# Forward transform of the last 64 rows: two matmuls on two quarters of the array become four matmuls on four quarters

## The chip, the core and the metric

The kernel runs on one core of a Trainium2 chip. The metric is the device time of one execution in microseconds (us); lower is better. Everything is float32. The engines go by the names of the profile: PE is the matrix engine (PEld its weight loads), DVE, ACT and POOL the vector, scalar and general engines, SP the engine that issues most DMAs. The array of PE is 128 rows by 128 columns. A matmul whose contraction has 64 rows and whose result has 64 rows fills a quarter of it; which quarter follows from the partitions that its inputs lie on and from those that its result goes to.

## What is computed

The reference runs two layers on an image batch `x` of 2 x 128 x 64 x 64. The first is a neighbourhood attention with layer norms and a small feed-forward part. The second is a full self-attention over the 4096 tokens of a batch, then a layer norm, and then a convolution over time with 16 long filters per branch, plus three short lags:

```
t = t + attention(ln(t))                         # 4096 tokens, 128 channels
u = ln(t)
U_plus, U_minus = causal FFT convolution of u with 16 filters   # per branch
t = t + sum_k s_k (U_plus_k @ M_plus_k + U_minus_k @ M_minus_k) + sum_i shift(u, i) @ M_u_i
```

One of four branches is chosen by a one-hot weighting, and the branches see the first 1, 1/2, 1/4 or 1/8 of the tokens.

## The kernel before

The convolution is done in blocks with a real transform of length `NC` = 320 (`CB` = 256 and `SB` = 64). The rows of the spectrum go through DRAM: the forward transform writes them to the buffer `us`, and the last stage loads them as `ut`. Beside `us` there is `gs` with the transformed filters.

The stages follow each other on the timeline like this:

- Up to about 440 us: the first layer, planned by hand, and the first work of the second.
- About 440 to 1332 us: the attention of batch 0 and then of batch 1, in `attention`. Its inner loop has PE do the products of tokens (L897), which ACT turns into weights `e` (L904); the weighted sums (L925, L950); and transposes of `e` (L911), which DVE copies out with their row sums to `et` (L914) before L925 takes them. After each inner step `fill()` puts in a slice of other work: the queue `urgent` first, then `steps`.
- About 1332 us to the end: the products in the transformed domain (L1304, L1316) and the way back.

Each time a chunk of 512 tokens has its final sum, `fill` gets a new generator `after` for it; there are 8 for each batch. Its slices are: transposes of the sum (L974), with a normalisation by DVE into `tt` (L979); the layer norm (L159, POOL's L160, and L177, which writes `z`); transposes of `z` (L188), copied by ACT into `zc` (L990); two slices with two matmuls each for the first 256 of the 320 rows of the transform (L1010), copied out by DVE and ACT in turn (L1012) and stored (L999); and a last slice for the remaining 64 rows (L1018, L1020), which is what the change touches. In batch 1's last steps, slices of `short_lags` (L1042, with DVE's L1049 and ACT's L1033) lie between.

In each slice `z2` holds 128 partitions. The two halves of 64 partitions, `q`, are two segments that are transformed separately; the transform matrix `tr` lies on both halves.

The buffers around the change: PSUM tiles `bank` come from a ring of six (`ps_m`) which all of these users share; the SBUF tiles `ub` come from a ring of three, and each `after` takes five of them; in the stage from about 838 to 920 us `filter_matrices` loads 32 blocks through two buffers `st` (L1103), which DVE scales and adds (L1106, L1108) and combines (L1119 to L1124). DVE's, ACT's and SP's queues are in order; the framework's scheduler sets that order in the attention stages.

Of the kernel before, what the change touches and what calls it, by code (L numbers as in the profile page):

```python
# [8 lines left out]
F32 = mybir.dt.float32  # L9
# [5 lines left out]
P = 128  # L15
# [66 lines left out]
SB = CB // SG  # L82
NC = CB + SB
# [9 lines left out]
def kernel(  # L93
# [16 lines left out]
    nc = tc.nc  # L110
# [14 lines left out]
    for c in range(4):  # L125
# [19 lines left out]
        out=flip, in_=flip, compare_op=ALU.not_equal, fill=1.0, base=1 - QT * QT, pattern=[[0, 2], [1, QT * QT]],  # L145
# [35 lines left out]
    def layernorm(dst, src):  # L181

        ln_apply(dst, src, ln_statistics(src))

    def transposed(ps, src):

        for j in range(src.shape[1]):
            nc.tensor.transpose(ps[:, j * P : (j + 1) * P], src[:, j, :], ident)  # L188
# [30 lines left out]
    with l0a:  # L219
# [6 lines left out]
        sp = l0a.enter_context(tc.tile_pool(name="l0_s", bufs=2))  # L226
# [27 lines left out]
        def table(ci, h, eng):  # L254
# [16 lines left out]
            out=gavg, in_=gavg, compare_op=ALU.is_ge, fill=0.0, base=0,  # L271
# [3 lines left out]
            out=gavg, in_=gavg, compare_op=ALU.is_ge, fill=0.0, base=3,  # L275
# [8 lines left out]
        for r in range(QT):  # L284
# [4 lines left out]
            rows_ = rev[r * QT : (r + 1) * QT].rearrange("p h n m -> p (h n) m")  # L289
# [563 lines left out]
    us = dram.tile([BINS, 2, SG, FB, NB, 2, P], F32, name="us")  # L853
    gs = dram.tile([BINS, 2, SG, GROW], F32, name="gs")

    with ap_:
        tp = ap_.enter_context(tc.tile_pool(name="l1_t", bufs=1, side="right"))
        ep = ap_.enter_context(tc.tile_pool(name="l1_e", bufs=8, side="right"))
        sp = ap_.enter_context(tc.tile_pool(name="l1_s", bufs=2, side="right"))
# [3 lines left out]
        def bank():  # L863
            return ps_m.tile([P, 512], F32, tag="bank", name="bank")
# [3 lines left out]
        tr = tp.tile([P, 2, NC], F32, name="tr")  # L868
# [98 lines left out]
        def after(b, c, part):  # L967

            n0 = 4 * c
            ph, f0 = divmod(n0, FB)  # L970
            par, h = divmod(ph, 2)
            pt = bank()
            for j in range(4):
                nc.tensor.transpose(pt[:, j * P : (j + 1) * P], xa[b][:, (n0 + j) * P : (n0 + j + 1) * P], ident)  # L974
            rden = sp.tile([P, 4], F32, tag="rden", name="rden")
            nc.vector.tensor_reduce(rden, part[:, n0 : n0 + 4, :], AX.X, ALU.add)
            nc.vector.reciprocal(rden, rden)
            for j in range(4):
                nc.vector.scalar_tensor_tensor(  # L979
                    tt[b][:, n0 + j, :], pt[:, j * P : (j + 1) * P], rden[:, j : j + 1], tt[b][:, n0 + j, :],  # L980
                    ALU.mult, ALU.add,
                )
            yield
            z = sp.tile([P, 4, P], F32, tag="z4", name="z4")
            layernorm(z, tt[b][:, n0 : n0 + 4, :])
            yield
            pt = bank()
            transposed(pt, z)
            s0 = 1 + h * (TH // 2)
            nc.scalar.copy(  # L990
                zc[:, par, s0 : s0 + TH // 2].rearrange("p (c f) -> p f c", f=FB)[:, f0 : f0 + 4, :],
                pt.rearrange("p (f c) -> p f c", f=4),
            )
            yield
            z2 = z.rearrange("p f d -> p (f d)")

            def store(m0, q, src):
                mn = min(P, NC - m0)
                nc.sync.dma_start(  # L999
                    out=us[m0 // 2 : (m0 + mn) // 2, :, 2 * h + q, f0 : f0 + 4, b, par, :].rearrange(  # L1000
                        "g r f d -> (g r) f d"
                    ),
                    in_=src.rearrange("p (f d) -> p f d", d=P),
                )

            for m0 in (0, P):
                for q in range(2):
                    rows_ = slice(q * SB, (q + 1) * SB)
                    pu = bank()
                    nc.tensor.matmul(pu, lhsT=tr[rows_, h, m0 : m0 + P], rhs=z2[rows_], start=True, stop=True)  # L1010
                    ub = sp.tile([P, 512], F32, tag="ub", name="ub", bufs=3)
                    (nc.scalar.copy if q else nc.vector.tensor_copy)(ub, pu)  # L1012
                    store(m0, q, ub)
                yield
            pu = bank()
            for q in range(2):
                rows_ = slice(q * SB, (q + 1) * SB)
                nc.tensor.matmul(pu[rows_], lhsT=tr[rows_, h, 2 * P : NC], rhs=z2[rows_], start=True, stop=True)  # L1018
            ub = sp.tile([P, 512], F32, tag="ub", name="ub", bufs=3)
            nc.scalar.copy(ub, pu)  # L1020
            for q in range(2):
                store(2 * P, q, ub[q * SB : (q + 1) * SB])
            yield

        def short_lags(b, h):
# [154 lines left out]
        def filler(b, steps, kept=None):  # L1180

            urgent, done = [], []

            def fill(c=None, part=None):
                if c is not None:
                    done.append(c)
                    urgent.append(after(b, c, part))
                    if len(done) % 4 == 0:
                        held = kept if kept is not None and len(done) == 4 else urgent
                        held.append(short_lags(b, len(done) // 4 - 1))  # L1190
                    return
                for queue in (urgent, steps):
                    while queue:
                        if next(queue[0], 0) is None:
                            return
                        queue.pop(0)

            return fill, urgent
# [291 lines left out]
```

## Time and profile before

| | |
|---|---|
| Median of 5 runs | 2244.25 us (2243.41 to 2245.45) |
| Profiled execution | 2244.14 us, its span 2242.4 us |
| PE busy | 2174.1 us, 97% of the span |
| DVE, ACT, POOL busy | 940.3, 780.5, 275.8 us |
| Mean granted PE clock | 0.99 |
| L1010 | 128 records of 64x512, 589 to 1219 ns |
| L1018 | 64 records of 64x512, 589 to 641 ns |
| L1012 | 32 copies by DVE (691 ns), 32 by ACT (585 ns) |
| L1020 | 16 copies by ACT (585 ns) |
| L999 | 64 stores of 256 KB, 32 of 128 KB |

How to read it: a float32 matmul of the program appears as two records, and matmuls that lie in different parts of the array overlap, so that records' durations don't add up; the distance between starts does. Ends of matmuls are modelled. In lines of the timeline, the first number is the start in us from the beginning of the span, the second the length in us up to the last end, then come engine, line, operation and tiles, and in brackets the idle time of the engine before it and what ended it. An engine with a q behind its name is its sequencer, which waits or issues.

### The profile page before, as it was taken

How to read it: one execution, taken by the hardware profiler on the slowest of the kernel's cores; microseconds unless marked ns; L12 is line 12 of the kernel's file. 1: busy time of each engine (PE TensorE's matmuls, PEld its weight loads, DVE VectorE, ACT ScalarE, POOL GpSimd, SP SyncE). 2: the span in 40 equal slices, each digit the busy share in tenths (PEclk: the TensorE clock that was granted, in tenths of full speed). 3: DMA queues.
4: the chain of work that ended last, by engine and by line, in shares of the span. 5: the costliest groups of instructions: out<-in, count | busy, mean ns of one | idle time of the engine just before them, and what ended most of it. 6: DMA issues, size and time to landing. Idle time of an engine off the chain costs nothing.

```text
span 2242.4 us, 31648 instructions
## 1 busy us (share of the span) xinstructions
PE 2174.1 (97%) x11888; PEld 1344.9 (60%) x11888; DVE 940.3 (42%) x3046; ACT 780.5 (35%) x1908; POOL 275.8 (12%) x353
## 2 busy tenths in 40 slices
PE   5899998999999999999999999999999999999998
PEld 3677775544454444544544447677677676767677
DVE  4799985434443346433333352222222323232323
ACT  2789883222332223222222332322322323232322
POOL 3367874200000000000000000000000000000000
PEclk8999998999999999999999999999999999999999
DMA  4222222011000016100000132212212122221101
GB/s 109 70 61 61 61 56 51 1 62 56 24 24 24 16 39 178 36 24 19 5 24 24 47 93 55 58 42 56 59 41 57 43 55 49 49 51 47 43 7 76
DMA packets 174810, 109.53 MB, mean 49 GB/s; under 512 B 26049, under 2 KB 159809, under 8 KB 174146
## 3 DMA queue, kind: packets, MB, share of 16 engines
q1 hardware_dynamic: 171818, 105.24, 17.9%
q10 hardware_dynamic: 2840, 2.27, 0.4%
q8 instruction: 94, 1.54, 0.3%
q14 instruction: 58, 0.48, 0.1%
HBM read 72.87 MB, written 34.60 MB: 48 GB/s over the span
## 4 chain that ended last, share of the span: by engine, by line
PE 86%; DVE 6%; POOL 3%; DMA 3%; ACT 1%; issue 1%; SPq 1%; DVEq 0%; ACTq 0%; POOLq 0%
PE acc L1316 25%; PE pc L1304 13%; PE bank L897 9%; PE own L925 9%; PE other L950 8%; PE bank L911 4%; PE bank L331 2%; PE py L1343 2%; PE bank L188 2%; PE bank L541 2%; PE bank L1042 1%; PE bank L1010 1%; DMA st<-in_m_minus_dram 1%; PE po L563 1%; DMA st<-in_m_plus_dram 1%; PE bank L505 1%
## 5 line engine op out<-in xcount | busy, mean ns | idle before, releaser
L1305 DVE COPY y<-pc 128x512 f32<-128x512 f32 x320 | 221.6, 692 | 351.5 <-PE pc L1304 347.8
L904 ACT ACTIVATE e<-bank 128x512 f32<-128x512 f32 x288 | 171.9, 597 | 553.3 <-PE bank L897 418.1
L897 PE MATMUL bank<-cm 128*128 128x512 f32 x576 | 298.6, 602 | 1.4 <-DVE y L652 1.4
L1316 PE MATMUL acc<-y,mpl 128*128 128x256 f32 x1280 | 292.1, 382 | 0.0
L1316 PE MATMUL acc<-y,mmi 128*128 128x256 f32 x1280 | 288.0, 379 | 0.0
L1304 PE MATMUL pc<-ct,ut 64*128 64x512 f32 x1280 | 285.2, 595 | 0.9 <-issue 0.9
L1316 PEld LDWEIGHTS acc<-y,mpl 128*128 128x128 f32 x1280 | 238.1, 190 | 59.4 <-issue 29.6
L1316 PEld LDWEIGHTS acc<-y,mmi 128*128 128x128 f32 x1280 | 242.6, 190 | 32.6
L1305 ACT COPY y<-pc 128x512 f32<-128x512 f32 x320 | 204.6, 639 | 87.2 <-PE pc L1304 87.2
L925 PE MATMUL own<-et,tok 128*128 128x512 f32 x448 | 227.1, 594 | 2.5 <-DVE part L914 2.5
L950 PE MATMUL other<-e,tok 128*128 128x512 f32 x448 | 228.6, 592 | 0.0
L914 DVE CUSTOM_DVE_ANT_0 et<-bank,one 128x512 f32<-128x512 f32 x224 | 145.6, 688 | 166.4 <-PE bank L911 166.3
L1304 PEld LDWEIGHTS pc<-ct,ut 64*128 64x128 f32 x1280 | 121.5, 187 | 145.8 <-issue 140.6
L1322 ACT COPY ob<-acc 128x256 f32<-128x256 f32 x40 | 23.8, 595 | 431.2 <-PE acc L1316 431.2
L925 PEld LDWEIGHTS own<-et,tok 128*128 128x128 f32 x448 | 84.4, 190 | 110.7 <-issue 72.1
L950 PEld LDWEIGHTS other<-e,tok 128*128 128x128 f32 x448 | 85.0, 190 | 106.6 <-issue 106.2
L1355 DVE TENSOR_TENSOR xa<-py,xa 128x512 f32<-128x512 f32 x32 | 22.1, 691 | 281.4 <-PE py L1343 281.4
L897 PEld LDWEIGHTS bank<-cm 128*128 128x128 f32 x576 | 95.7, 193 | 73.8 <-issue 44.7
L911 PEld LDWEIGHTS bank<-ident,e 128*128 128x128 f32 x896 | 103.5, 142 | 57.2 <-issue 43.4
L160 POOL TENSOR_TENSOR ln_rs<-ln_rs,mhalf 128x4 f32<-128x4 f32 x24 | 24.3, 1011 | 848.4 <-DVE ln_rs L159 848.4
L528 ACT ACTIVATE p<-p,mn 128x196 f32<-128x196 f32 x256 | 114.4, 449 | 21.5 <-DVE mn L518 13.4
L911 PE MATMUL bank<-ident,e 128*128 128x128 f32 x896 | 117.8, 275 | 0.0
(199 smaller groups left out, 2311.9 us busy)
## 6 DMA issues: line engine op xcount, KB each, us to landing
ut<-us SPq DMA_DIRECT2D x80, 256.0 KB
us<-ub SPq DMA_DIRECT2D x64, 256.0 KB
vw<-vd SPq DMA_DIRECT2D x256, 49.0 KB
ct<-gs SPq DMA_DIRECT2D x160, 72.0 KB
ct<-gs SPq DMA_DIRECT2D x160, 64.0 KB
gs<-sum SPq DMA_DIRECT2D x20, 256.0 KB
vd<-v SPq DMA_DIRECT2D x128, 32.0 KB
st<-in_m_plus_dram SPq DMA_DIRECT2D x16, 256.0 KB
```

What stands on the lines that cost most here:

```text
L188: nc.tensor.transpose(ps[:, j * P : (j + 1) * P], src[:, j, :], ident)
L331: nc.tensor.matmul(pl, lhsT=wg[:, lo : lo + P], rhs=zT, start=True, stop=True)
L528: nc.scalar.activation(p, p, AF.Exp, bias=t[name + "mn"][:, h : h + 1], scale=-1.0, accum_out=t["den"][:, u, h : h + 1],)
L897: nc.tensor.matmul(ps, lhsT=cm[b][:, n * P : (n + 1) * P], rhs=cm[b][:, chunk(c)], start=True, stop=True)
L904: nc.scalar.activation(e, ps, AF.Exp, bias=0.0, scale=ASCALE, accum_out=part[:, n, c : c + 1])
L911: nc.tensor.transpose(pt[:, k * P : (k + 1) * P], es[k][:, m * P : (m + 1) * P], ident)
L914: nc.vector.tensor_tensor_reduce(et, pt, one, 1.0, 0.0, ALU.mult, ALU.add, part[:, n, a : a + 1])
L925: nc.tensor.matmul(own, lhsT=tok[b][:, n, :], rhs=e, start=first, stop=last)
L950: nc.tensor.matmul(other, lhsT=tok[b][:, 4 * CHUNKS[a] + j, :], rhs=es[j], start=(j == 0), stop=(j == 3))
L1304: nc.tensor.matmul(pc, lhsT=ut[fp, b, par, :], rhs=cv_[fp], start=True, stop=True)
L1305: (nc.scalar.copy if f else nc.vector.tensor_copy)(y[:, 4 * f : 4 * f + 4, :, par, b * 2 * FB + q : (b + 1) * 2 * FB : 2], pc.rearrange("p ...
L1316: nc.tensor.matmul(acc, lhsT=(mmi if l else mpl)[:, k, :], rhs=y[:, 1::2, k, ::-1, :] if l else y[:, 0::2, k, :, :], start=(l == 0 and k = ...
```

## The change

Before, the last slice of `after` runs one matmul for each half `q`: 64 rows in, 64 rows out, 512 columns moving. The result of `q` goes to the partitions of `q` of one bank. ACT copies the bank to one `ub`, and two stores of 128 KB send it off.

After, each matmul is split in two by its moving columns (`i`: 256 columns each). The result of `i` goes to the partition half `i`, and that of `q` to a bank of its own, so that the four matmuls lie in the four quarters of the array. Two banks are taken in place of one. Half of the `ub` is copied by DVE (`q` = 0), the other half by ACT (`q` = 1), with 256 columns each, and four stores of 64 KB follow. The arithmetic is the same.

```diff
-                mn = min(P, NC - m0)
...
-            pu = bank()
-            for q in range(2):
-                rows_ = slice(q * SB, (q + 1) * SB)
-                nc.tensor.matmul(pu[rows_], lhsT=tr[rows_, h, 2 * P : NC], rhs=z2[rows_], start=True, stop=True)
-            ub = sp.tile([P, 512], F32, tag="ub", name="ub", bufs=3)
-            nc.scalar.copy(ub, pu)
-            for q in range(2):
-                store(2 * P, q, ub[q * SB : (q + 1) * SB])
+            banks = [bank() for q in range(2)]
+            for i in range(2):
+                for q in range(2):
+                    rows_ = slice(q * SB, (q + 1) * SB)
+                    nc.tensor.matmul(
+                        banks[q][i * 64 : (i + 1) * 64, 0:256], lhsT=tr[rows_, h, 2 * P : NC],
+                        rhs=z2[rows_, i * 256 : (i + 1) * 256], start=True, stop=True,
+                    )
+            ub = sp.tile([P, 512], F32, tag="ub", name="ub", bufs=3)
+            for q in range(2):
+                (nc.scalar.copy if q else nc.vector.tensor_copy)(ub[:, q * 256 : (q + 1) * 256], banks[q][:, 0:256])
+                for i in range(2):
+                    nc.sync.dma_start(
+                        out=us[P:, :, 2 * h + q, f0 + 2 * i : f0 + 2 * i + 2, b, par, :].rearrange("g r f d -> (g r) f d"),
+                        in_=ub[i * 64 : (i + 1) * 64, q * 256 : (q + 1) * 256].rearrange("p (f d) -> p f d", d=P),
+                    )
```

The order of the instructions on PE and POOL is otherwise the same. On DVE and SP the scheduler's order also changes from about 850 to 920 us: three pairs of L914 and some neighbours stand at other places among the operations of `filter_matrices`.

## The prediction

> **What bounds the kernel now.** I read the page first, for the bound and the chain of waits; then the lines that the change touches; then the timeline of one step, of the two places where PE waits for DVE, and of the only other line that uses parts of the array in both directions.
>
> ```profile
> PE 2174.1 (97%) x11888; PEld 1344.9 (60%) x11888; DVE 940.3 (42%) x3046; ACT 780.5 (35%) x1908; POOL 275.8 (12%) x353
> ...
> PE 86%; DVE 6%; POOL 3%; DMA 3%; ACT 1%; issue 1%; SPq 1%; DVEq 0%; ACTq 0%; POOLq 0%
> ```
>
> PE is busy for 97% of the span and carries 86% of the chain: time taken off PE reaches the end wherever PE does not then wait for something that has not moved. The timeline of the first step:
>
> ```profile
> 483.68 1.07 PE L1018 MATMUL bank<-z,tr 64*64 64x512 f32 x4
> ...
> 484.69 0.98 PE L911 MATMUL bank<-ident,e 128*128 128x128 f32 x7
> 484.85 0.58 ACT L1020 COPY ub<-bank 128x512 f32<-128x512 f32 x1 [0.75 <-ACT e L904]
> 485.38 0.69 DVE L914 CUSTOM_DVE_ANT_0 et<-bank,one 128x512 f32<-128x512 f32 x1 [2.82 <-PE bank L911]
> ```
>
> A float32 matmul is two records (x4 for two matmuls). The two matmuls lie in the two diagonal quarters and run together; from their start to that of L911 PE spends 1.01 us. There are 16 such steps, starting at 483.7, 584.5, 661.4, 722.9, 783.8, 820.7, 848.0, 870.6, 976.1, 1061.1, 1134.2, 1195.2, 1244.1, 1281.0, 1301.4 and 1314.9.
>
> **The matmuls.** A column streams in 0.855 ns (the chain has 64 records of L1316, 256 columns each, in 14.01 us: 0.219 each). So 1.01 = 2 passes x 512 columns (0.876) + 0.13 for changing the array's division and the second weights. After: if all four quarters run at once, 2 passes x 256 columns (0.438) + the overhead. Nearest row, from the timeline of the first layer:
>
> ```profile
> 36.50 0.59 PE L505 MATMUL bank<-kT,qT 32*64 32x196 f32 x16
> 37.02 0.38 PE L720 MATMUL bank<-v_sb,w_sb 128*128 128x1 f32 x2
> ```
>
> Eight matmuls on four row groups x two column groups, each pair on the same rows with other moving data and the other half of one bank, as in the change. PE gets to L720 after 0.52 us. Two passes of 196 columns are 0.335, so the overhead is 0.18; taking turns on the same rows would need four passes, 0.67 of streaming alone. So they run at once. With overheads of 0.13 (L1018) to 0.18 (L505) the step becomes 0.57 to 0.62; I take 0.59, with twice L1018's loads but half of L505's: 0.42 saved, bounds 0.39 to 0.44. Over 16 steps, 6.7 us if all of it arrived.
>
> The Trainium skill's page "TensorE: Matmul & The Clock Gate", section "Part 3: Packing small matmuls — row/col tiling", speaks against this: a weight load overlaps running matmuls only when its row group differs. By it the two column quarters of one row half would take turns, and the sum would be that of the first rival below. The L505 row disagrees.
>
> **Evictions and stores.** Removed: 16 ACT copies (585 ns). Added: 16 ACT and 16 DVE copies of half the size, ACT at most 585, DVE between 341 (L177, 128 columns) and 691 (L1012, 512); I take 460, with 0.37 until the next may start. ACT and DVE are busy 35% and 42%. In an ordinary step the DVE half would run at about 484.4 and be done before L914, which in the changed order comes next and could start at 484.96: nothing while it is ready, and a late copy would delay L914 and the L925 behind it. SP gets 32 issues more, at 0.36 to 0.61 each; SP is idle in most of this stage, so they cost something only where loads queue behind them (below). Each step takes one bank more of the ring of six. In the order of the changed program the nearest misses are L1018's second bank (freed 0.65 before use, 1301.4) and L1042 at 1305.90 (freed 1.02 before), against 0.42 by which PE comes earlier: no stall.
>
> **The new wait.** The fifth ub of a step reuses the buffer of its second, so it waits for that store. Until now only ACT waited. Now the DVE half waits in front of everything queued on DVE. By the semaphore updates that store lands about 5.1 us after the step's first L1010, 483.70 in the first step, before the matmuls end; in the steps at 584.5 and 1061.1 it lands 1.5 later, which holds L914 by 0.2, against 1.1 of slack: nothing. In the step at 1301.4 the matmuls come early and the store late:
>
> ```profile
> 1301.39 1.08 PE L1018 MATMUL bank<-z,tr 64*64 64x512 f32 x4
> ...
> 1303.53 1.13 DVE L979 SCALAR_TENSOR_TENSOR tt<-bank,rden,tt 128x128 f32<-128x128 f32 x4 [1.94 <-PE bank L974]
> ...
> 1305.05 0.58 ACT L1020 COPY ub<-bank 128x512 f32<-128x512 f32 x1 [0.17 <-DMA us<-ub]
> ...
> 1307.17 1.12 DVE L177 TENSOR_SCALAR z<-tt,ln_mv,ln_rs 128x128 f32<-128x128 f32 x4
> ...
> 1308.48 0.60 PE L188 MATMUL bank<-ident,z 128*128 128x128 f32 x4
> ```
>
> In the changed order the DVE half stands ahead of L979. If the store lands as here, 1305.0, L979 starts at 1305.36, 1.83 late; L159, POOL and z follow, z at 1309.0, and the fourth L188 leaves PE 1.46 later than now. This landing is 3.7 after issue where most take 2.8; with 2.8 it is 1304.0, L979 0.87 late, the fourth L188 0.50 late. I take +0.5; bounds -0.42 (nothing held) and +1.5. That step's saving is gone either way.
>
> **838 to 920, the filter matrices.** 32 loads go through two st buffers; DVE takes each, and the next load waits for that:
>
> ```profile
> 850.16 0.75 DVE L1108 SCALAR_TENSOR_TENSOR mmi<-st,wt,mmi 128x512 f32<-128x512 f32 x1 [1.14 <-DMA st<-in_m_minus_dram]
> 851.72 0.75 DVE L1108 SCALAR_TENSOR_TENSOR mmi<-st,wt,mmi 128x512 f32<-128x512 f32 x1 [0.81 <-DMA st<-in_m_minus_dram]
> ...
> 858.67 1.10 PE L188 MATMUL bank<-ident,z 128*128 128x128 f32 x4 [2.95 <-DVE z L177]
> ```
>
> PE waits for z here, so the saving of the step at 848.0 is lost. The changed order also moves work. (a) The DVE half, 0.26 net ahead of L1119, and one L1124 of 0.20 now behind L979: z 0.06 later. (b) SP issues four stores (0.65 apart), the first behind the DVE half (852.9, now 851.47): the next st load goes out at 855.5 for 852.84, but DVE wants it at 859.7; inv at 858.6 for 855.94, so L1272 waits until about 862.3, hidden behind L1012, which needs PE until 862.7. (c) Behind the next step the four stores put one load 1.75 late, and three L914 pairs now stand ahead of the last scalings of a block, each holding the next load by 1.2 us: by the last block the loads run 4.2 late. (d) The same moves bring those pairs forward. Pair by pair, with the load times of now: the L925 at 893.60 (waited 1.22) gets its et 0.9 earlier, that at 900.60 1.25 later, 912.61 0.2 later. The last pair ends its first half at 919.55, now 917.5, for the L925 at 918.74: PE leaves the stage 0.85 later than now, with the saving of the step at 870.6 gone too. Bounds -0.4 (loads only 3 late) and +3 (pairs not helped by their new places).
>
> **Sum.** 13 steps x 0.417 = 5.4; less 0.85 and 0.5: 4.1. The profiled execution took 2244.14 (span 2242.4 and 1.7 around it), 0.1 under the median of 2244.25; 2244.14 - 4.1 = 2240.0, 2240.1 beside the median. Bounds: 16 x 0.44 = 7.0 gained at best, 2237.2; 13 x 0.39 - 3 - 1.5 = 0.6 at worst, 2243.6. A difference of 0.2%, 4.5 us, is about what a measurement of this kernel can tell from no change: the edges are 2239.8 and 2248.7.
>
> **Rivals.** *The quarters of one row half take turns* (the change doesn't do what it says): four passes of 256 columns in a row, 0.876, the overhead of 0.13, and two reloads more at 0.05 (L505's second passes start 0.218 after the first, 0.168 of it streaming), 1.11 in all, 0.10 lost per step: 1.6 + 0.85 + 0.5, 2247.1, slower. It decides if PE's step stays over 1 us. For it: nothing in the trace; against it: L505. Chance 0.06. *All of it arrives*: the stage at 838 comes out even and no z is late, 5.4 to 6.7 gained, about 2238.2. For it: the st loads' landings vary by over 1 us and the pairs move forward. Against: the DVE half's wait at 1301 is in the order. Chance 0.25. *The filter chain becomes the path*, slower than before: in 838 to 920 every load goes out behind a store, a half copy or a pair. PE pays what the last et is late beyond 1.15 of slack; at 4.2 late and 2.3 brought forward that is 0.8. It eats the 4.9 left elsewhere once the loads run 8.3 late, about one more load turn (3.1) and a half; at 12 late, a turn lost in each of the last three blocks, 2248. For it: L1108's waits; against: the last two blocks have no stores. Chance 0.08. The forecast has 0.61, with its own range 2238.6 to 2242.
>
> **How the numbers follow.** About a third of the forecast's chance lies under 2239.8 (0.20), and nearly all of the second rival's: faster 0.43. Slower by over 4.5 us needs the third, and a hair of the first: 0.07. Same 0.50. Range 2236.9 to 2244: best bound to just past the worst.
>
> **What would show it.** Right: L1018's successor with x8 records of 64x256 and the next PE operation 0.55 to 0.62 after its start; the ordinary steps each 0.4 shorter; DVE's half copy near 1301 ended by "DMA us<-ub" and L188 late behind z; st loads later, L925 near 918 waiting for L914. Wrong: a PE step of 1 us; PE leaving the 838 stage more than 3 later; PE waiting for a bank behind L1018.

## The result

Over 29 runs the changed kernel took 2242.0 us in the median (2237.74 to 2243.98), over 49 runs the kernel before 2244.31 (2239.96 to 2248.39). The ratio is 0.9988, 95% interval 0.9983 to 0.9993: some 2.7 us less, inside the 0.2% that was counted as no change, and 1.9 us over the forecast of 2240.1. The profiled execution of the change took 2239.94 us (span 2238.1). Its page:

```profile
PE 2166.8 (97%) x11952; PEld 1342.3 (60%) x11952; DVE 946.2 (42%) x3062; ACT 776.9 (35%) x1908; POOL 275.8 (12%) x353
...
PE 86%; DVE 6%; POOL 3%; DMA 3%; ACT 1%; SPq 1%; issue 1%; DVEq 0%; ACTq 0%; POOLq 0%
```

PE has 7.3 us less of busy time, 2166.8 for 2174.1, and still carries 86% of the chain. The timeline of the first changed step:

```profile
480.94 0.66 PE L1019 MATMUL bank<-z,tr 64*64 64x256 f32 x8
...
481.53 1.09 PE L911 MATMUL bank<-ident,e 128*128 128x128 f32 x8
481.71 0.42 DVE L1025 COPY ub<-bank 128x256 f32<-128x256 f32 x1 [1.89 <-PE bank L1019]
481.74 0.37 ACT L1025 COPY ub<-bank 128x256 f32<-128x256 f32 x1 [0.39 <-ACT e L904]
...
482.23 0.69 DVE L914 CUSTOM_DVE_ANT_0 et<-bank,one 128x512 f32<-128x512 f32 x1
```

Four matmuls are eight records of 256 columns; L911 follows 0.59 us after their start, where it took 1.01. All 16 steps show 0.59. Both half copies run beside each other and are done before L914.

The step near 1301 is at 1297.63 now:

```profile
1297.63 0.66 PE L1019 MATMUL bank<-z,tr 64*64 64x256 f32 x8
...
1299.73 0.42 DVE L1025 COPY ub<-bank 128x256 f32<-128x256 f32 x1 [1.90 <-DMA us<-ub]
...
1300.07 1.11 DVE L979 SCALAR_TENSOR_TENSOR tt<-bank,rden,tt 128x128 f32<-128x128 f32 x4
...
1303.71 1.11 DVE L177 TENSOR_SCALAR z<-tt,ln_mv,ln_rs 128x128 f32<-128x128 f32 x4 [0.40 <-POOL ln_rs L160]
...
1304.30 0.90 PE L188 MATMUL bank<-ident,z 128*128 128x128 f32 x4
```

DVE stood 1.90 us until a store had landed, with L979 queued behind, and z came late. In the stage with the filter matrices:

```profile
846.02 0.75 DVE L1116 SCALAR_TENSOR_TENSOR mmi<-st,wt,mmi 128x512 f32<-128x512 f32 x1 [2.16 <-DMA st<-in_m_minus_dram]
847.54 0.75 DVE L1116 SCALAR_TENSOR_TENSOR mmi<-st,wt,mmi 128x512 f32<-128x512 f32 x1 [0.77 <-DMA st<-in_m_minus_dram]
...
854.59 1.16 PE L188 MATMUL bank<-ident,z 128*128 128x128 f32 x4 [4.49 <-DVE z L177]
...
871.15 1.12 PE L925 MATMUL own<-et,tok 128*128 128x512 f32 x2 [0.66 <-DVE part L914]
...
889.87 1.13 PE L925 MATMUL own<-et,tok 128*128 128x512 f32 x2 [0.38 <-DVE part L914]
...
898.11 1.13 PE L925 MATMUL own<-et,tok 128*128 128x512 f32 x2 [1.07 <-DVE part L914]
```

PE came 5.2 us earlier to this stage than before, but only 4.1 earlier to L188 of z. It waited 4.49 us for z (before: 2.95), and then three times for L914. Before, it waited for L914 twice:

```profile
893.60 1.13 PE L925 MATMUL own<-et,tok 128*128 128x512 f32 x2 [1.07 <-DVE part L914]
...
912.61 1.12 PE L925 MATMUL own<-et,tok 128*128 128x512 f32 x2 [0.67 <-DVE part L914]
```

Counted from the stage's first L1010, the last of these waits ends at 73.99 us there. In the change it is the wait at 898.11, which ends at 64.69 and belongs to the L925 that stood at 900.60 before, without a wait.

**Where the time went.** I cut both timelines at the first L1010 (L1009 in the change) of each of the 16 steps and subtracted. The 7th, 8th and 15th steps are those at 848.0, 870.6 and 1301.4 of the kernel before (there the times are of L1018). The last column is a second profile of the same changed kernel, from the second group of runs below. All in us, change minus before:

| Stretch | Forecast | Change | Change again |
|---|---|---|---|
| Start to 1st step | 0 | -2.74 | -2.80 |
| 1st to 7th (six steps) | -2.5 | -2.46 | -2.22 |
| 7th to 9th | +0.85 | +2.23 | +2.30 |
| 9th to 15th (six steps) | -2.5 | -2.47 | -2.52 |
| 15th to 16th | +0.5 | +1.58 | +0.61 |
| 16th to the end | -0.4 | -0.41 | -0.42 |
| 1st step to the end | -4.1 | -1.53 | -2.25 |

Two things stand out. The first row is not the change's: nothing is changed there, and over the 14 profiles of this case the first step starts anywhere from 475.67 to 479.08, in kernels with and without the change. It would be a mistake to compare spans of single profiles here: the profiled execution's 2239.94 us lies beside the forecast of 2240.1 only because of it, which is luck. And the stretch from the 7th to the 9th step gives back most of what is lost.

### The profile page after: what moved, and what is told of

It is laid out like the page before. It is cut to its first block, busy times and chain, and to the rows that moved or that the text cites. A ratio compares the mean times of both kernels' runs of the same rounds, so it can differ in the third digit from the quotient of the medians.

```text
span 2238.1 us, 31885 instructions
## 1 busy us (share of the span) xinstructions
PE 2166.8 (97%) x11952; PEld 1342.3 (60%) x11952; DVE 946.2 (42%) x3062; ACT 776.9 (35%) x1908; POOL 275.8 (12%) x353
## 4 chain that ended last, share of the span: by engine, by line
PE 86%; DVE 6%; POOL 3%; DMA 3%; ACT 1%; SPq 1%; issue 1%; DVEq 0%; ACTq 0%; POOLq 0%
PE acc L1324 25%; PE pc L1312 13%; PE bank L897 10%; PE own L925 10%; PE other L950 8%; PE bank L911 4%; PE py L1351 2%; PE bank L331 2%; PE bank L188 2%; PE bank L1050 2%; PE bank L1009 1%; PE bank L541 1%; DMA st<-in_m_minus_dram 1%; PE po L563 1%; PE bank L505 1%
## 5 line engine op out<-in xcount | busy, mean ns | idle before, releaser
L925 PE MATMUL own<-et,tok 128*128 128x512 f32 x448 | 227.4, 594 | 2.8 <-DVE part L914 2.8
L914 DVE CUSTOM_DVE_ANT_0 et<-bank,one 128x512 f32<-128x512 f32 x224 | 145.6, 688 | 134.0 <-PE bank L911 133.0
L925 PEld LDWEIGHTS own<-et,tok 128*128 128x128 f32 x448 | 84.1, 190 | 112.0 <-issue 71.8
L911 PEld LDWEIGHTS bank<-ident,e 128*128 128x128 f32 x896 | 103.2, 141 | 51.7 <-issue 42.0
L911 PE MATMUL bank<-ident,e 128*128 128x128 f32 x896 | 117.5, 274 | 0.0
```

The lines of the kernel that those rows point to most:

```text
L911: nc.tensor.transpose(pt[:, k * P : (k + 1) * P], es[k][:, m * P : (m + 1) * P], ident)
L914: nc.vector.tensor_tensor_reduce(et, pt, one, 1.0, 0.0, ALU.mult, ALU.add, part[:, n, a : a + 1])
L925: nc.tensor.matmul(own, lhsT=tok[b][:, n, :], rhs=e, start=first, stop=last)
```

## The experiments

Three theories stood at the start. **A**: the loss from the 7th to the 9th step and at the 15th comes from DVE's half copy, through what is queued behind it and the order that follows. **B**: it comes from the clock. After an idle time PE can stream at half speed for a while, and the change makes PE idle longer in front of z. In the windows view (us, PE busy, granted clock, DMA share, GB/s) of the changed kernel the two stretches around 1293.46 read:

```profile
1290.05:1293.46 3.41, 1.81 (x8) 1.00 0.00 0
1293.46:1296.87 3.41, 3.41 (x9) 0.50 0.00 0
```

1.6 us of idle, then 3.41 us at a clock of 0.50, which do 1.7 us of work. From the first step on, up to the end of the span where every profile has one, the kernel before shows one such record, of 3.41 us after the 2.95 us of idle; the change shows 6.83 us after the 4.49, and this one. **C**, a third: the stores on SP, now four for the last slice, hold up the filter loads.

The kernels ran in three groups: the first four below, the next four, the last four. Each group has its own runs of the kernel before, with medians of 2242.21, 2243.39 and 2243.31, and ratios refer to these.

### ACT only: both half copies by ACT

```diff
-                (nc.scalar.copy if q else nc.vector.tensor_copy)(ub[:, q * 256 : (q + 1) * 256], banks[q][:, 0:256])
+                nc.scalar.copy(ub[:, q * 256 : (q + 1) * 256], banks[q][:, 0:256])
```

> The four matmuls of the change stay, but ACT copies both halves, so DVE's queue is that of before (one pair of neighbours swapped). Theory A (what is missing of the forecast is given back by DVE: its half copy in front of L979 and L914, and the L914 pairs that moved): 15 steps x 0.41 = 6.2 gained, about 2238.2 against 2244.3. Theory B (it is given back by PE's clock, because PE idles longer before z near 858 and gets more windows at half speed, 1.7 us each): 15 x 0.41 - 1.7 to 3.4 = 2.8 to 4.5 gained, 2239.8 to 2241.5. In both the L1019 steps read 0.59 to the next PE operation, and no L979 stands behind a DVE half.

Measured: 2238.14 us, ratio 0.9983 (0.9974 to 0.9992). The time is the one that A named, but A and B reckoned from 2244.3, and this group's kernel before took 2242.21. As ratios A stands for 0.9973 and B for 0.9980 to 0.9988, so the time lies in B's range. DVE's instructions are back in the order of the kernel before, but for one pair of neighbours. From the 7th to the 9th step it takes 132.59 us (before 132.36, change 134.59), from the 15th to the 16th 10.15 (before 10.56, so this step's 0.41 now arrives). There the timeline shows DVE free for L979, and z ahead of PE:

```profile
1296.94 1.13 DVE L979 SCALAR_TENSOR_TENSOR tt<-bank,rden,tt 128x128 f32<-128x128 f32 x4 [1.52 <-PE bank L974]
...
1301.89 0.60 PE L188 MATMUL bank<-ident,z 128*128 128x128 f32 x4
```

L979 waits for its transposes, not for a store, and L188 (0.60 for four, none held up) waits for nothing. ACT waits for the store instead (0.37 us), with nothing urgent behind it. So A holds for the 15th step. For the other stretch A and B stay open.

### Eviction only: the old matmuls with the new copies and stores

```diff
-            nc.scalar.copy(ub, pu)
-            for q in range(2):
-                store(2 * P, q, ub[q * SB : (q + 1) * SB])
+            for i in range(2):
+                cs = slice(i * 256, (i + 1) * 256)
+                (nc.scalar.copy if i else nc.vector.tensor_copy)(ub[:, cs], pu[:, cs])
+                for q in range(2):
+                    nc.sync.dma_start(
...
+                        in_=ub[q * SB : (q + 1) * SB, cs].rearrange("p (f d) -> p f d", d=P),
+                    )
```

> The two matmuls of before in one bank, with the change's DVE half, ACT half and four stores: what the eviction costs by itself. Theory A: DVE's queue and the stores cost 2.5 to 3.5, about 2247.3. Theory B: 0.5 at the step near 1300 and about 0.9 in the stage from 838 to 920, no longer idle than before at z, so 1.0 to 1.5, about 2245.5. If it is 2244.3 or less, the eviction costs nothing and the missing part is all in what PE does with the time.

Measured: 2243.68, ratio 1.0008 (0.9999 to 1.0017). As ratios A stands for 1.0013 and B for 1.0005, so the time does not tell them apart. From the 15th to the 16th step 11.69, so 1.13 lost, all of it the wait for the store:

```profile
1302.63 0.43 DVE L1022 COPY ub<-bank 128x256 f32<-128x256 f32 x1 [3.13 <-DMA us<-ub]
1302.97 1.12 DVE L979 SCALAR_TENSOR_TENSOR tt<-bank,rden,tt 128x128 f32<-128x128 f32 x4
...
1307.10 0.75 PE L188 MATMUL bank<-ident,z 128*128 128x128 f32 x3 [0.56 <-DVE z L177]
```

The stretch from the 7th to the 9th step does not lose here: 131.38, a microsecond less than before, although DVE's instructions stand nearly in the order of the change (seven of some 200 elsewhere). So neither the new copies nor that order alone fix what the stretch costs. What differs from the change is that z came at 20.00 us after the 7th step's first L1010 (change 20.68, before 19.64), and that PE then ran at full clock.

### ACT queue: the change with the second half's stores issued by ACT

```diff
-                    nc.sync.dma_start(
+                    (nc.scalar if q else nc.sync).dma_start(
```

> The change, with the two stores of ACT's half issued from ACT's queue, so that SP issues two per step as before. If the stores on SP are a good part of what is missing (the loads of the filter matrices queue behind them): 1 or more faster than the change, 2241 or less. Theories A and B, for which the st loads in the stage at 838 are late for the L914 pairs' sake or don't matter: within 0.7 of the change, 2241.5 to 2242.5.

Measured: 2240.23, under the 2241 that C expected, but beside this group's 2242.21 the ratio is 0.9988 (0.9979 to 0.9997), that of the change itself. In its profile the 7th to the 9th step take 132.32, with yet another order of DVE's instructions; the 15th to the 16th 11.19. DVE keeps its half copy at 848.0 here as well, and the stretch does not lose. The profile speaks for C, the times don't. The run "ACT both" below decides it.

### Kept busy: three matmuls for nothing in front of one wait

```diff
+            if b == 0 and c == 7:
+                idle = bank()
+                for _ in range(3):
+                    nc.tensor.matmul(idle, lhsT=ident, rhs=one, start=True, stop=True)
             pt = bank()
             transposed(pt, z)
```

> The change, with three more 128x128 by 512 matmuls (0.87 each) whose result nobody reads, put ahead of the transposes of z in the step near 858 alone: PE works for 2.6 us where it waited for z. Theory B: the idle time falls under what lowers the clock, PEclk stays at 1.00 there, and 1.7 to 3.4 come back: 2238.6 to 2240.3. Theory A: PE waits for z as long as before, and nothing comes back or some 0.3 is lost: 2242.0 to 2242.5.

Measured: 2241.44, ratio 0.9995 (0.9986 to 1.0004). The three filled 2.6 us, but 2.38 of idle was left, and a record at half speed (3.41) followed as before. This run does not test B; the next three do.

### The change again

> The changed kernel once more, as the base of this group. In its profile of before, PE at full speed does 5.7 us less from the first changed step to the end; 1.9 us more of idle time and 2.7 us more of half-speed streaming take most of that back. Both theories: 0.9980 to 0.9992 of the kernel before. Theory A (queue order and waits give the rest back): the idle before L188 near 854.6 is 4 to 4.5 us again, and that alone explains the difference of runs. Theory B (half-speed stretches after long idle): that idle is there too, and the half-speed records number one to three after the first changed step, differing between executions.

Measured: 2240.91, ratio 0.9992 (0.9983 to 1.0001). Its profile is the last column of the table. The idle time in front of L188 is 4.42, the stretch from the 7th to the 9th step 134.66: what that stretch loses is the same in both profiles. The record at half speed at 1293.46 is missing, and the 15th step loses 0.97 less.

### Filled change

```diff
+            idle = {(0, 6): 1, (0, 7): 4, (1, 6): 1}.get((b, c), 0)
+            if idle:
+                spare = bank()
+                for _ in range(idle):
+                    nc.tensor.matmul(spare, lhsT=ident, rhs=one, start=True, stop=True)
             pt = bank()
             transposed(pt, z)
```

> The change plus matmuls into a bank that nobody reads, put where PE waits for z before L188: one (0.86 us) before the 7th step of the first half, four (3.4 us) before its 8th, one before the 7th step of the second half. They lie in idle time of 1.6, 4.5 and 1.6 us. Theory B: no half-speed record between the first changed step and the last store, so 1.5 to 3 us less than the change alone. Theory A: z comes when it came, the time is that of the change within 0.5 us.

Measured: 2242.47, ratio 0.9995 (0.9986 to 1.0004), so no gain; the interval overlaps with that of the change again. The timeline shows where the next wait lies:

```profile
852.79 3.60 PE L991 MATMUL bank<-one,ident 128*128 128x512 f32 x8
858.12 1.10 PE L188 MATMUL bank<-ident,z 128*128 128x128 f32 x4 [1.73 <-DVE z L177]
...
866.96 1.60 PE L925 MATMUL own<-et,tok 128*128 128x512 f32 x2 [2.21 <-DVE part L914]
```

PE passes z without the slow stretch, and then waits 2.21 us for L914, which DVE gets to no earlier. (This wait was followed by a record at half speed of its own, and DVE's order is not that of the change: 34 of some 200 instructions stand elsewhere.)

### Filled before

The same edit in the kernel before, with three matmuls for the four.

> The kernel before plus the same filling, with three matmuls (2.6 us) in place of four, since PE idles 2.95 us there. Theory B: the kernel before has about one half-speed stretch of 3.41 us after its 2.95 us of idle, and now and then one after the two idles of 1.6 us; without them it is 1.5 to 2 us shorter, ratio 0.9991 to 0.9993, and the filled change is 3.5 to 4 us below it (5.7 of matmuls less 1.9 of idle). Theory A: ratio 1.0000 within 0.0003.

Measured: 2243.17, ratio 1.0005 (0.9996 to 1.0014). From the 7th to the 9th step 133.76: 1.40 more than before, without one changed copy or store. The filling alone moved about ten of DVE's instructions there, and z came 20.54 us after the 7th step's first L1010 instead of 19.64. The half-speed record came again, after 2.22 us of idle, so B was not put to the test.

### Filled ACT only

> The version in which ACT copies both halves, with the filling of the filled change (one, four, one matmul). Theory B: the profile shows no half-speed record after the first changed step, and 1 to 2.5 us come off the 0.9983 of that version: 0.9973 to 0.9979 of the kernel before. Theory A: 0.9983 again, since the copies are already off DVE.

Measured: 2238.83, ratio 0.9977 (0.9968 to 0.9986), the lowest ratio of all. It lies in B's range, but the interval covers A's 0.9983 as well. Here the filling worked as meant: no half-speed record is left in this stretch. The windows view of the 7th to the 9th step, ACT only first and then the filled one:

```profile
834.30:966.89 132.59, 126.56 (x411) 0.97 0.33 92
```

```profile
833.89:966.89 133.00, 128.13 (x419) 1.00 0.33 93
```

A clock of 0.97 against 1.00: two half-speed records against none. In ACT only PE streams for 5.8 us inside those records, so that B, if PE were the bound throughout, would make the filled one 2.9 us shorter. It is 0.4 us longer. This does not rule B out, because the two differ in more than the clock. In ACT only the slow PE reaches DVE: the L1009 behind z takes twice as long as usual,

```profile
858.19 2.08 PE L1009 MATMUL bank<-z,tr 64*128 64x512 f32 x4
```

and DVE stands 2.12 us before its copy L1011, with the filter loads behind it. In the filled one (where L1009 is L1014) this is gone:

```profile
854.54 1.01 PE L188 MATMUL bank<-ident,z 128*128 128x128 f32 x4 [1.39 <-DVE z L177]
...
857.20 1.13 PE L1014 MATMUL bank<-z,tr 64*128 64x512 f32 x4
...
862.40 1.12 PE L925 MATMUL own<-et,tok 128*128 128x512 f32 x2 [1.32 <-DVE part L914]
...
871.23 1.12 PE L925 MATMUL own<-et,tok 128*128 128x512 f32 x2 [0.54 <-DVE part L914]
...
890.45 1.12 PE L925 MATMUL own<-et,tok 128*128 128x512 f32 x2 [0.88 <-DVE part L914]
```

Its filter loads go out up to 1.45 us earlier than in ACT only (30.54 us after the 7th step's first L1009 against 31.99). But two of them land 4.09 and 3.98 us after their issue, where the same two took 2.98 and 2.92 in ACT only, and the lead is gone. DVE's order differs as well, in 14 instructions. So the loss of time to the clock is neither shown nor excluded here. What the two have in common is the bound: in both the last wait for L914 ends about 56 us after the 7th step's first L1009 (56.14 and 56.56), and from there to the 9th step both take 76.44. What decides the stretch is when DVE, behind its loads, gets to that L914.

This kernel has DVE's other instructions in exactly the order of the filled change. It takes 133.00 where that one takes 134.95 (with one half-speed record in it): with the order held, DVE's half copies and that record make up to 2 us, from one profile each.

### DVE's half copy at one of the two steps

Both half copies by ACT at the 7th and the 15th step, the others as in the change ("DVE at 870.6"):

```diff
+                on_act = (b, c) in ((0, 6), (1, 6))
-                (nc.scalar.copy if q else nc.vector.tensor_copy)(ub[:, q * 256 : (q + 1) * 256], banks[q][:, 0:256])
+                (nc.scalar.copy if q or on_act else nc.vector.tensor_copy)(ub[:, q * 256 : (q + 1) * 256], banks[q][:, 0:256])
```

The names in the following expectations are their own: theory C there is A narrowed to the copy at 848.0, not the C of the stores.

> The change, but at two steps (the one whose last matmuls stood at 848.0 in the kernel before, and the one at 1301.4) ACT copies both halves; DVE keeps its half at the other fourteen, the one at 870.6 among them. The scheduler then leaves DVE's other instructions in the order of the kernel before. Measured so far, from the 7th step's first matmul to the 9th's: before 132.4 us, change 134.6 to 134.7 (two profiles), ACT only 132.6; from the 15th step to the 16th: before 10.56, change 11.17 (without a half-speed stretch), ACT only 10.15. Theory C (DVE's half copy at 848.0, in front of the accumulation of the filter matrices that makes z late, with the order of DVE that follows from it, costs the 2.0 us): 132.6 and 10.15 again, and 0.9976 to 0.9984 of the kernel before, like ACT only. Theory D (DVE's half copy at the step at 870.6 costs it, or both together): 133.5 to 134.7, and 0.9984 to 0.9988.

Its counterpart, with `((0, 7), (1, 6))` in place of `((0, 6), (1, 6))` ("DVE at 848.0"):

> The counterpart: ACT copies both halves at the steps at 870.6 and 1301.4, DVE keeps its half at the one at 848.0 and at the other thirteen. DVE's other instructions stand in the order of the change but for two. Theory C: from the 7th step to the 9th 134 to 134.7 us as in the change, 10.15 from the 15th to the 16th, and 0.9984 to 0.9989 of the kernel before. Theory D: 132.6 to 133.5, and 0.9977 to 0.9984.

Measured: DVE at 870.6 took 2238.8, ratio 0.9983 (0.9974 to 0.9992); DVE at 848.0 took 2240.84, ratio 0.9991 (0.9982 to 0.9999). Windows of the 7th to the 9th step, in this order:

```profile
834.85:968.32 133.47, 128.39 (x412) 0.96 0.33 92
```

```profile
833.87:968.93 135.06, 129.18 (x411) 0.96 0.33 91
```

Both are longer than theory C expected (132.6 and 134 to 134.7); 133.47 lies nearer to D. Both have a third half-speed record, near 835, after the 1.6 us of idle before the 7th step, where ACT only and the change had none. It may be the reason, but Eviction only has such a record too (837.87) and is the shortest of all. Beside each other, at the same clock, the two differ by 1.59 us. This points to the step at 848.0, and the ratios fit C. But the two kernels differ in DVE's order too (25 of some 200 instructions), so that the copy and the order that follows from it are not told apart, and the intervals of the ratios overlap. From the 15th to the 16th step both take 10.15: with ACT copying there the loss of that step is gone, whatever happens elsewhere.

### ACT both: both copies by ACT, the second half's stores from ACT's queue

The edits of "ACT only" and "ACT queue" together.

> ACT copies both halves everywhere, and the two stores of the second half are issued from ACT's queue, so that SP issues six stores for a step as in the kernel before, not eight. DVE's order is that of the kernel before. In the ACT only version SP issued the fifth filter load of the stage 16.4 us after the 7th step's first matmul, 14.2 in the kernel before. If the two issues more on SP hold up the loads: 14.2 to 15.5, the stretch from the 7th to the 9th step 132.0 to 132.4, and 0.9974 to 0.9982. If they do not: 132.6, and 0.9983 as before.

Measured: 2238.21, ratio 0.9982 (0.9973 to 0.9991), that of ACT only. The load that the expectation counts as the fifth (it is the first of the stage's second block) went out 15.9 us after the 7th step's first L1009 in place of 16.4, and z came no earlier (21.26 against 20.60). The stretch took 133.92, with the same third half-speed record as the two before. Load and stretch miss what theory C of the stores expected, and the ratio is that of ACT only, so nothing here speaks for C. The 133.92 shows something else: ACT only, with DVE's instructions in the same order but for one pair, took 132.59. Profiles of kernels that hardly differ on DVE lie 1.3 us apart in this stretch.

### Rows first: the four matmuls in another order

```diff
-            for i in range(2):
-                for q in range(2):
+            for q in range(2):
+                for i in range(2):
```

> The change with the order of its four small matmuls swapped: the two column quarters of one row half behind each other, then the two of the other, in place of alternating halves. Read from the distance between the first of the four and the next L911. If quarters on the same rows run at once whatever the order: 0.59 to 0.62 us as in the change. If a load of weights for rows that are streaming has to wait for them: the second matmul waits for the first, and the step becomes 0.8 to 1.0 us.

One execution took 2239.9. The timeline of its first step:

```profile
482.53 0.66 PE L1019 MATMUL bank<-z,tr 64*64 64x256 f32 x8
483.13 1.09 PE L911 MATMUL bank<-ident,e 128*128 128x128 f32 x8
```

0.59 (from start to start, before rounding) in all 16 steps, as in the change. The two column quarters of the same rows run at once in either order. The swap also moved DVE's instructions in the filter stage: 21 of some 200 stand elsewhere than in the change, and only 4 elsewhere than in ACT only. The stretch from the 7th to the 9th step is 133.52, 1.1 less than the change's with the same copies and the same clock of 0.97, and 0.9 more than that of ACT only with nearly the same order. Taken at their word the order makes about 1 us and the copies about 1, but both are smaller than the 1.3 between ACT only and ACT both.

### The runs together

| DVE's half copy at 848.0 | Ratios |
|---|---|
| not there (ACT only, filled ACT only, ACT both, DVE at 870.6) | 0.9983, 0.9977, 0.9982, 0.9983 |
| there (change, again, ACT queue, DVE at 848.0, kept busy, filled) | 0.9988, 0.9992, 0.9988, 0.9991, 0.9995, 0.9995 |

The intervals of single kernels (about 0.0009 to either side) overlap; the ratios of the two rows do not. Their means, 0.9981 and 0.99915, lie 0.001 apart, 2.3 us. Up to 1.0 us of that is the 15th step, which none of the first row loses; of the second row only DVE at 848.0 doesn't lose it either. The filled kernels widen the gap: without them the means are 0.9983 and 0.9990, 1.6 us apart, and what is left for the copy at 848.0 is less than the times can tell. ACT only is the simplest version that is clear of the kernel before: 0.9983, where the change has 0.9988 and 0.9992. That it is ahead of the change is likely, but the intervals overlap.

## Why the prediction was right, and where it was off

The verdict, within 0.2% of no change, was the likeliest of the three, and 2242.0 lies in the range. The forecast itself lies 1.9 us below, and the table says in which term.

- **The matmuls**: 0.59 forecast, 0.59 measured, 16 times; 13 steps at 0.41 arrive, as the sum had it. The overhead, 0.155 beside 0.438 of streaming, lies between the 0.13 and 0.18 of the two rows that it was taken from. The Trainium skill's page "TensorE: Matmul & The Clock Gate", section "Part 3: Packing small matmuls — row/col tiling", lets a weight load overlap running matmuls only where its row group differs; the measured 0.59, in either order of the four, shows no such wait between quarters of one row half. In the trace of rows first the second quarter of the same rows has its load start 7 ns after the first one's, while the first matmul streams. That the quarters would take turns was the prediction's own inference from that sentence. The first rival (turns, 1.11) is out.
- **Copies and stores**: DVE's half took 416 to 426 ns (460 forecast), ACT's 372 (at most 585). No bank held PE up behind L1019.
- **The new wait at the 15th step**: forecast +0.5, measured +0.61 in the second profile and +1.13 with the old matmuls (which includes no saving: the change's 0.61 and its lost 0.41 make 1.02). The mechanism is as described: DVE's copy is ended by the store, L979 stands behind it, z is late. Taking the copy off DVE removed it. The first profile shows 1.58; its extra 0.97 goes with a half-speed record there, which the forecast did not have.
- **838 to 920**: forecast +0.85, measured +2.23 and +2.30. This is the term that was mis-sized, though not beyond its bound of 3. Part (a) had z 0.06 later; it came 1.04 later (measured from the 7th step). Nearly all of that is the load of the L1116 shown at 846.02, which DVE got 1.06 later: it was issued 0.25 later and took 3.89 us to land in place of 3.07. I had taken all load times from the one profile of before. In all the 13 other profiles, that of the filled kernel before among them, z came 0.36 to 1.66 later than in that one: its loads seem to have landed early there, and the difference is not all the change's. Part (c) had the loads 4.2 late by the last block; the last one was issued 6.28 later. Part (d) went wrong with it. The pair for the L925 at 893.60 (its wait is 1.07 us in the view, not 1.22) was to come 0.9 earlier; counted from the 7th step it came 1.5 later. That for 900.60 was to come 1.25 later and came 3.9 later, that for 912.61 0.2 later and came 2.1 later. The moved pairs stood behind loads that were themselves late. So the path of the forecast is not the one that was taken either: the wait that was to set the 0.85, for the last pair at the L925 near 918, did not occur. The one that counted was that for 900.60. The prediction also left out that PE streams at half speed behind z, for 3.4 us before and for 5.4 in the change; DVE waits for copies of what PE makes there, so that this can be a part of the 2.2.
- **The rivals**: all of it arriving (0.25) needed that stretch to come out even. This did not happen to the change, but nearly to ACT only (+0.23, and no late z at the 15th step): 4.9 us from the first step on. The filter chain as the path names the right place, but far from its price: the chain ate 2.2 us besides the 0.8 of the two steps, where the rival needed all of the 4.9.

What stays open is how the 2 us of that stretch split among DVE's half copy, the order of DVE's instructions, the clock and the landings of the loads. The filled pair, with the same order of DVE, puts up to 2 on the copies; rows first against the change, with the same copies, puts 1 on the order. Against both, Eviction only and ACT queue have the half copy at 848.0 and lose nothing there; both have z earlier than the change (20.00 and 20.16 against 20.68) and less half-speed streaming behind it (none and 3.0 us against 5.4). The two profiles of the change agree within 0.1 us, but no run held all else fixed, since the scheduler sets the order anew after every edit. A fourth buffer for `ub`, which would take away the wait at the 15th step and leave the copy on DVE, was not tried.

## What to carry to other kernels

Work that goes from one engine to another should go to the one with nothing urgent queued behind it: at the 15th step ACT's copies cost nothing, while DVE's stood in front of the chain that PE waits for. A stage in which PE waits several times for a chain on another engine can give back what is saved ahead of it, as it did here with the shorter matmuls and with the filling; compare such stages by stretches from marker to marker, in more than one profile, before a time of a single landing goes into a sum.

## What was not expected of the hardware

Records at half speed come in multiples of 3.41 us, at distances that are multiples of it too, while the program's start lies anywhere on that grid. An idle time of 1.60 us in front of L188 was followed by one in some profiles (near 835 in three of the last group, near 1293 in the first profile of the change) and not in others (both places in the second profile). The Trainium skill's page "TensorE: Matmul & The Clock Gate", section “Part 1: The HAM clock gate (the "warmup" mystery)”, has a free-running window of about 3.4 us, which agrees, and a return to half speed after at least one idle window, which does not: 1.60 us of idle, half a window, was enough. At the 15th step such a record cost 0.97 us (12.14 with it and 11.17 without), not the 1.7 of its lost streaming.
